# Two attention images per transfer: layouts of keys, offsets, results and matrices, and three picked rows per read, in a deformable attention kernel

## The chip, the cores and the metric

The kernel runs on one core of one Trainium2 chip. Its time is the device time of one execution in microseconds (us); of several executions the median counts. The profile is one further execution under the hardware profiler.

## The reference

A network of two layers works on an image batch of shape (2, 64, 64, 256) in fp32. Each layer adds an attention block and then a mixture-of-experts feed-forward block to its input. The change touches the first layer's attention block alone, which is cut to its core here (B = 2 images, G = 8 groups of HC = 32 channels, K = 9 sampling points):

```python
qkv = _dwconv_nhwc(x @ qkv_w + qkv_b, dw_w, dw_b)      # q, k_map, v_map
mask = jnp.einsum('bchw,oc->bohw', _pconv_nchw(q_nchw, mask_pconv_w), mask_w) + mask_b
for g in range(G):
    off = jnp.einsum('bchw,oc->bohw', _pconv_nchw(q_nchw, off_pconv_w[g]), off_w[g]) + off_b[g] + base[g]
    k_list.append(_flow_warp(k_map[:, sl], off) * mask[:, None])
    v_list.append(_flow_warp(v_map[:, sl], off) * mask[:, None])
attn = softmax(einsum('bgpc,bgpkc->bgpk', qh, k))
out = einsum('bgpk,bgpkc->bgpc', attn, v) @ proj_w + proj_b
```

`base[g]` holds the nine points of a 3 x 3 grid with spacing 2g+1. `_flow_warp` samples a map bilinearly at the pixel's own place plus the offset, with the place clipped to the image. Behind this block follow the first feed-forward block, the second layer's windowed attention and its feed-forward block.

## The kernel before

The kernel is one program. What matters here runs from about 660 to 2880 us of the profiled execution, in two stages.

**Maps.** A depthwise convolution turns the projected q, k and v into maps in DRAM. For q it runs on DVE (`dwconv`), and ACT copies each piece into `q0` or `q1` (L366); SP stores them in `qd` (L368, L370). For v it also runs on DVE, followed by transposes on PE (`ps_t`, L380) and stores to `vd`. For k PE computes it with diagonal weights (`ps_k`, L424), ACT moves the PSUM tile to `km` (L429), and SP stores it in `kd` with a border of repeated columns on both sides (L434, L436). From `q0` and `q1` PE computes the offsets and the mask (`ps_off`, L447 and L448), which ACT copies (L452) and SP stores in `offd` (L453). `offd` has the shape [128, 153, 64]: rows (y, b), then 144 offsets and 9 mask values in the order (g, kx, ky, two), then x.

**Attention.** Because the offsets are smaller than one pixel (a flag `far` tells when they aren't, and another path then runs instead), no gather is needed: every sample is a weighted sum of the 3 x 3 pixels around its grid point. A group g goes through three lanes:

- `group_dots`: SP reads queries and keys (`qt`, L544; `kt`, L554), PE multiplies each column of queries with three columns of keys (`dot`, L564), ACT moves the products to `stage` (L571) and stores them in DRAM as `dots` (L580). `dots` has the shape [y, b, 6, 64, 3, 32]: for each row of queries and image, six blocks (three grid columns by two halves of x), 64 rows of keys, three key columns, 32 queries.
- `group_weights`: SP reads the offsets (`tents`, L632) and picks from `dots` those key rows that each query row needs (`lk`, L660; in `read`, L663, for each of the three grid rows three neighbouring rows). DVE adds the bias (L637), ACT and DVE make the bilinear weights ("tents"), DVE sums the picked products to logits (L694 to L708) and takes the softmax. DVE then makes `wy` (L733), and POOL multiplies it out to the weights `wt` (L740) and stores them along diagonals of a DRAM matrix `wd` (L773). Before it does so it clears that matrix's old diagonals with zeros from `none` (L788, `clean`).
- `group_values`: SP reads the values (`raw`, L859) and DVE spreads them to a block-diagonal `vt` (L861). POOL loads bands of `wd` to one of two buffers `mat` (L868, `load`), PE multiplies `vt` with `mat` into `acc` (L890, `add`), ACT copies a half's result (L899) and stores it in `od` (L903). There are six loads and six adds for a group, four in the last, group 0.

`static_attention` (L456) runs values of one group, weights of the next and dots of the one after that side by side. It puts the steps of the three lanes in one list by a position for each (`lanes`, L503 to L517); a scheduler of the framework then orders each engine's instructions from that list by its own estimates, so the order on an engine isn't that of the source. The groups come in the order 1 to 7, then 0. All DMAs that SP issues share one queue, those of ACT a second and those of POOL a third.[...]

The two images are kept apart in most transfers: one DMA for b = 0 and one for b = 1, as in the load of the matrices:

```python
def load(n):
    h, kx, _ = runs[n]
    for b in range(B):
        for y in range(0, H, BAND):
            lo, hi = band(g, y)
            nc.gpsimd.dma_start(mats[n % 2][H * b + y : H * b + y + BAND, lo:hi], wd[y : y + BAND, b, 2 * kx + h, lo:hi])
```

Such a load fills 16 partitions (BAND = 16), eight of them a matrix. At the end `project_out` reads `od` to `oT` (L931) and multiplies with `proj_w`.

Of the kernel before, what the change touches and what calls it, by code (L numbers as in the profile page):

```python
# [31 lines left out]
P = 128  # L32
# [89 lines left out]

def _shape_constants():
# [9 lines left out]
    grid = np.concatenate([grid.reshape(P, NOFF), np.zeros((P, K), np.float32)], 1)  # L133
# [31 lines left out]
    fold = np.concatenate([fold, own], 1)  # L165
# [15 lines left out]
class Net:  # L181
# [80 lines left out]
    def static_maps(self, maps, sort):  # L262
# [10 lines left out]
        with ExitStack() as ctx:  # L273
# [73 lines left out]
            with tc.tile_pool(name="mpad", bufs=2) as pads, tc.tile_pool(name="mq", bufs=1) as qp, \  # L347
# [12 lines left out]
                for b in range(B):  # L360
                    for j in range(CC):
                        for y in range(0, H, YC):
                            cv = kp.tile([P, YC, W], F32, name="cv")
                            self.dwconv(cv, padded("pad", j, b, y, YC), j, 0, YC)
                            to = q1[:, :, y : y + YC, b] if j else q0[:, 1 : W + 1, 1 + y : 1 + y + YC, b]
                            nc.scalar.copy(to.rearrange("p x y -> p y x"), cv)  # L366
# [43 lines left out]
                for j in range(CC):  # L410
# [5 lines left out]
                    for b in range(B):  # L416
                        km = kp.tile([P, W, H], F32, name="km", bufs=1)
                        for y in range(0, H, 8):
# [3 lines left out]
                            for tap in range(9):  # L422
# [7 lines left out]
                                km[:, :, y : y + 8].rearrange("p x y -> p y x"), ps, AF.Identity,  # L430
                                bias=bias,
                            )
                        to = kd[j * P : (j + 1) * P, b]
                        nc.sync.dma_start(to[:, BORDER : BORDER + W, :], km)  # L434
                        for at, src in ((0, 0), (BORDER + W, W - 1)):
                            nc.sync.dma_start(  # L436
                                to[:, at : at + BORDER, :], km[:, src : src + 1, :].to_broadcast([P, BORDER, H])
                            )
                XO = 8
                for x8 in range(0, W, XO):  # L440
                    off = op.tile([P, NOM, XO], F32, name="off")
                    for x in range(x8, x8 + XO, 2):
# [9 lines left out]
                        nc.scalar.copy(off[:, :, x - x8 : x - x8 + 2].rearrange("p n x -> p x n"), ps)  # L452
# [3 lines left out]
    def static_attention(self, maps, od, far):  # L456
# [7 lines left out]
        with ExitStack() as ctx:  # L464
# [12 lines left out]
            edge = one.tile([P, len(FOLDS) + B], F32, name="edge")  # L477
# [9 lines left out]
            def masks():  # L487

                masks = offd[:, NOFF:, :].rearrange("(y b) (kx ky) x -> b y ky kx x", b=B, kx=3)
                for b in range(B):  # L490
                    for ky in range(3):
                        nc.sync.dma_start(mask[H * b : H * b + H, 3 * ky : 3 * ky + 3, :], masks[b, :, ky])
                v = mask.rearrange("p (ky kx) x -> p ky kx x", ky=3)
                ob = self.row("offb")[:, NOFF:].rearrange("p (kx ky) -> p ky kx", kx=3)
                nc.vector.tensor_tensor(v, v, ob.unsqueeze(3).to_broadcast([P, 3, 3, W]), ALU.add)
                for t in mats + [none, pools["vt"]]:
                    nc.gpsimd.memset(t, 0.0)

            for n in range(-2, G):
                lanes = []  # L500
                if n >= 0:
                    g = ORDER[n]
                    lanes.append((lambda f: 0.12 + 0.88 * f, self.group_values(g, vd, wd[n % 2], mats, none, sums, od, pools)))  # L503
# [7 lines left out]
                if n + 2 < G:  # L511
                    g = ORDER[n + 2]
                    lanes.append((lambda f: 0.95 * f, self.group_dots(g, qd, kd, edge[:, len(FOLDS) :], dots, pools, n < 0)))
# [12 lines left out]
    def group_dots(self, g, qd, kd, own, dots, pools, alone):  # L526
# [22 lines left out]
        def keys(h, dx):  # L549
            box[h, dx] = kt = two.tile([P, XQ + 2, H], F32, name="kt", bufs=3)  # L550
            for j in range(2):
                for b in range(B):
                    x, p0 = BORDER + XH * h + XQ * j + dx, 64 * j + 32 * b
                    nc.sync.dma_start(kt[p0 : p0 + HC], kd[g * HC : (g + 1) * HC, b, x : x + XQ + 2])  # L554
# [45 lines left out]
    def group_weights(self, g, offd, mask, low, edge, s, wd, none, pools):  # L600
# [24 lines left out]
        def offsets():  # L625
            src = offd[:, g * 2 * K : (g + 1) * 2 * K, :].rearrange(
                "(y b) (kx ky two) x -> b y two ky kx x", b=B, kx=3, ky=3
            )
            for b in range(B):
                for i in range(2):  # L630
                    for ky in range(3):
                        nc.sync.dma_start(t5[H * b : H * b + H, 1, i, 3 * ky : 3 * ky + 3, :], src[b, :, i, ky])  # L632

        def bias(i):
            v = t5[:, 1, i].rearrange("p (ky kx) x -> p ky kx x", ky=3)
            ob = self.row("offb")[:, g * 2 * K : (g + 1) * 2 * K].rearrange("p (kx ky two) -> p two ky kx", kx=3, ky=3)
            nc.vector.tensor_tensor(v, v, ob[:, i].unsqueeze(3).to_broadcast([P, 3, 3, W]), ALU.add)  # L637
# [7 lines left out]
        def pick(to, dy, first, blocks, n):  # L645

            for b in range(B):
                y = 0
                while y < H:
                    ky = min(max(y + dy, 0), H - 1)  # L650
                    inside = 0 <= y + dy < H
                    end = min(H, H - dy) if inside else (-dy if dy < 0 and y < -dy else H)
                    m = end - y
                    if m > 16:
                        m -= m % 16
                    src = bass.AP(
                        s.tensor, s.offset + y * stride + b * (stride // B) + first * block + ky * line,
                        [[stride + (line if inside else 0), m], [block, blocks], [1, n * XH]],
                    )
                    nc.sync.dma_start(to[H * b + y : H * b + y + m], src)  # L660
                    y += m

        def read(ky):  # L663
            box[ky] = lk = two.tile([P, 3, 6, 3, XH], F32, name="lk")
            for sy in range(3):
                pick(lk[:, sy].rearrange("p k s x -> p k (s x)"), (ky - 1) * r + sy - 1, 0, 6, 3)

        def read_near():
            flat = two.tile([P, 27 * W], F32, name="ln", tag="lk")
            box["all"] = lk = flat[:, 0 : 25 * W].rearrange("p (y h s x) -> p y h s x", y=5, h=2, s=5)  # L670
            box["l"] = two.tile([P, 3, 6, 3, XH], F32, name="l4", tag="lk")
# [7 lines left out]
        def in_x(ky):  # L679
            tx = t5[:, :, 0, 3 * ky : 3 * ky + 3, :]  # L680
            if near:
                lk, box[ky] = box["all"], box["l"]
                for sy in range(3):
                    out = box[ky][:, sy].rearrange("p (k h) s x -> p h k s x", h=2)
# [8 lines left out]
            for sy in range(3):  # L693
                nc.vector.tensor_tensor(box[ky][:, sy], box[ky][:, sy], tx, ALU.mult)  # L694

        def sum_x(ky, i):
            l = box[ky].rearrange("p y k s x -> p (y k) s x")
# [1792 lines left out]
```

## Time and profile before

| what | value |
| --- | --- |
| median of 3 runs | 5861.54 us (5854.24 to 5861.91) |
| profiled execution | 6110.76 us, span 6109.0 us, granted TensorE clock 0.796 |
| PE, PEld, DVE, ACT, POOL busy in the span | 67%, 47%, 40%, 19%, 24% |
| maps | about 660 to 1190 us |
| attention, dots alone | 1190 to 1425 us |
| attention, all three lanes | 1425 to 2410 us |
| attention, the last groups' values | 2410 to 2880 us |
| output projection | 2880 to 3060 us |
| everything behind (not touched) | 3060 to 6109 us |

The busy shares are means over the whole program, in which stages with quite different limits follow each other. A change in the attention must be read from windows of the profile within it: how busy each engine and the 16 DMA engines are there, what the engines wait for, and in which order POOL, SP and ACT issue their work. An engine's idle time costs nothing unless the end of the stage depends on it.

The groups that carry the stage, from the groups of instructions between 1190 and 2880 us (line, engine, operation, names, shapes, count; busy us and mean ns of one; idle us before them and what ended the idle time):

```profile
L890 PE MATMUL acc<-mat,vt 128*64 128x192 f32 (+2 forms) x3680 | 491.7, 439 | 255.9 <-DMA mat<-wd 182.0 <-DMA wd<-wt 32.8 <-DVE vt L861 26.1
L564 PE MATMUL dot<-kt,qt 64*128 64x192 f32 x2944 | 408.4, 411 | 479.1 <-ACT stage L571 320.8 <-DVE stage L571 61.7 <-DMA kt<-kd 43.5
L868 POOL DMA_DIRECT2D mat<-wd x368 | 179.8, 494 | 590.5 <-PE acc L890 390.5 <-DMA wd<-none 88.1 <-DMA mat<-wd 61.4
L773 POOL DMA_DIRECT2D wd<-wt x170 | 167.6, 991 | 143.6 <-issue 49.4 <-DMA wd<-wt 36.4 <-DMA mat<-wd 31.0
L740 POOL TENSOR_TENSOR wt<-tents,wy 128x192 f32<-128x192 f32 x216 | 128.5, 626 | 198.6 <-DVE wy L733 189.3 <-DMA wd<-wt 9.0
```

### The profile page before, as it was taken

The page shows a single profiled execution, that of the slowest core. Times are in us where ns is not written, and L with a number is a line of the kernel's source. Part 1 is how long each engine was busy: PE and PEld are TensorE (multiplying, and loading weights), DVE is VectorE, ACT ScalarE, POOL GpSimd, SP SyncE. Part 2 cuts the span into 40 slices and gives each one's busy share as a digit, 9 for nine tenths or more (in the row PEclk, how much of TensorE's full clock was granted, in tenths as well). Part 3 has the DMA queues.
Part 4 walks back from the last instruction along what each step waited for, and adds up shares of the span by engine and source line. Part 5 has one row for each costly group of instructions (what it writes and reads, how often), then busy time and mean ns, then how long its engine had stood idle before and what let it go on. Part 6 is the DMA issues. An engine that isn't in the chain of part 4 may idle for free. (4 is left out here: it accounts for less than half of the span.)

```text
span 6109.0 us, 63383 instructions
## 1 busy us (share of the span) xinstructions
PE 4115.2 (67%) x22123; PEld 2876.5 (47%) x22123; DVE 2467.9 (40%) x5464; ACT 1154.1 (19%) x2302; POOL 1470.7 (24%) x1792
## 2 busy tenths in 40 slices
PE   7877688758265566354625680499947877769982
PEld 4655245745243444233412340388824444458872
DVE  6788985043121202220423473011155555532223
ACT  2110121122122222000100000122213343322210
POOL 1000001123342232443155414300062111110025
PEclk8776799868577777677867795699967888879986
DMA  6333367968678897787320001577621000058875
GB/s 179 97 102 113 99 171 148 66 152 179 126 159 175 176 188 155 120 142 126 84 13 4 4 2 64 173 225 223 194 86 40 22 21 22 21 184 263 263 235 159
DMA packets 775144, 759.72 MB, mean 124 GB/s; under 512 B 443959, under 2 KB 658935, under 8 KB 759317
## 3 DMA queue, kind: packets, MB, share of 16 engines
q1 hardware_dynamic: 576992, 412.37, 26.8%
q0 software_dynamic: 87008, 200.21, 16.9%
q10 hardware_dynamic: 110804, 142.87, 8.1%
q8 instruction: 182, 2.98, 0.2%
q14 instruction: 158, 1.29, 0.1%
HBM read 461.72 MB, written 296.60 MB: 124 GB/s over the span
## 5 line engine op out<-in xcount | busy, mean ns | idle before, releaser
L564 PE MATMUL dot<-kt,qt 64*128 64x192 f32 x2944 | 408.4, 411 | 479.1 <-ACT stage L571 320.8
L890 PE MATMUL acc<-mat,vt 128*64 128x192 f32 (+2 forms) x3680 | 491.7, 439 | 255.9 <-DMA mat<-wd 182.0
L564 PEld LDWEIGHTS dot<-kt,qt 64*128 64x128 f32 x2944 | 355.5, 235 | 535.7 <-ACT stage L571 340.5
L1658 PE MATMUL ps_h<-xgT,w1t 128*128 128x256 f32 x2240 | 545.0, 391 | 41.8 <-DVE xgT L1653 17.6
L1391 PE MATMUL ps<-oh,ol 128*128 128x512 f32 (+1 forms) x864 | 363.2, 584 | 240.8 <-issue 150.5
L1666 PE MATMUL ps_y<-w2t,hT 128*128 128x256 f32 x2240 | 513.9, 383 | 7.5 <-issue 4.4
L890 PEld LDWEIGHTS acc<-mat,vt 128*64 128x64 f32 x3680 | 310.3, 163 | 441.1 <-issue 318.1
L1658 PEld LDWEIGHTS ps_h<-xgT,w1t 128*128 128x128 f32 x2240 | 417.6, 193 | 122.8 <-DVE xgT L1653 26.2
L1666 PEld LDWEIGHTS ps_y<-w2t,hT 128*128 128x128 f32 x2240 | 430.0, 192 | 69.1 <-issue 5.2
L1661 ACT ACTIVATE hT<-ps_h,b1t 128x256 f32<-128x256 f32 x560 | 258.6, 473 | 846.4 <-PE ps_h L1658 756.7
L571 ACT COPY stage<-dot 128x384 f32<-128x384 f32 x640 | 269.5, 495 | 745.6 <-PE dot L564 295.2
L1669 DVE TENSOR_TENSOR y<-ps_y,b2t 128x256 f32<-128x256 f32 x280 | 118.8, 424 | 648.2 <-PE ps_y L1666 493.7
L1391 PEld LDWEIGHTS ps<-oh,ol 128*128 128x128 f32 x864 | 179.6, 212 | 424.0 <-issue 319.9
L868 POOL DMA_DIRECT2D mat<-wd x368 | 179.8, 494 | 590.5 <-PE acc L890 390.5
L424 PE MATMUL ps_k<-padk,diag 128*128 128x512 f32 x576 | 266.1, 621 | 76.4 <-issue 50.2
L260 DVE SCALAR_TENSOR_TENSOR cv<-pad,colt,cv 128x2048 f32<-128x2048 f32 x128 | 293.8, 2347 | 1.3
L2286 POOL DMA_INDIRECT xs<-tn,sloti x128 | 124.2, 971 | 638.9 <-DVE slot L2284 592.7
L1753 POOL DMA_INDIRECT back<-ys,back_row x128 | 123.3, 964 | 621.9 <-DVE run L2271 548.6
L1275 PE MATMUL psc<-oh,ol 128*128 128x64 bf16 x1792 | 235.0, 305 | 55.6 <-DVE oh L1273 55.6
L1275 PEld LDWEIGHTS <-ol 128*128 128x128 bf16 x1792 | 224.9, 148 | 94.0 <-issue 54.9
L333 PE MATMUL ps_q<-xT,wq 128*128 128x512 f32 x384 | 217.7, 708 | 44.5 <-ACT stage L337 33.2
L1651 PE MATMUL ps_x<-ident,xg 128*128 128x128 f32 x560 | 85.0, 275 | 225.4 <-DMA xg<-xs 225.4
(401 smaller groups left out, 6112.7 us busy)
## 6 DMA issues: line engine op xcount, KB each, us to landing
w1t<-in_W SPq DMA_DIRECT2D x140, 512.0 KB
w2t<-in_W SPq DMA_DIRECT2D x140, 512.0 KB
xg<-xs SPq DMA_DIRECT2D x140, 256.0 KB
ys<-y ACTq DMA_DIRECT2D x140, 256.0 KB
kt<-kd SPq DMA_DIRECT2D x184, 144.0 KB
pr<-stage SPq DMA_DIRECT2D x16, 1584.0 KB
mat<-wd POOLq DMA_DIRECT2D x112, 192.0 KB
mat<-wd POOLq DMA_DIRECT2D x64, 288.0 KB
```

The lines of the kernel that those rows point to most:

```text
L260: nc.vector.scalar_tensor_tensor(out, src, w, out, ALU.mult, ALU.add)
L333: nc.tensor.matmul(ps.rearrange("p a b -> p (a b)"), lhsT=wq[:, k, c * P : (c + 1) * P], rhs=xT[:, k, :], start=(k == 0), stop=(k == CC - 1),)
L424: nc.tensor.matmul(ps.rearrange("p a b -> p (a b)"), lhsT=diag[:, tap, :], rhs=pad[:, at : at + 8, tap % 3 : tap % 3 + W], start=(tap == 0 ...
L564: nc.tensor.matmul(ps[jj][:, i, :], lhsT=qt[at, i0 + i].rearrange("p y b -> p (y b)"), rhs=kt[at, i0 + i : i0 + i + 3, :].rearrange("p s y ...
L571: (nc.vector.tensor_copy if alone and jj else nc.scalar.copy)(box["d"][:, :, :, x : x + 2], ps[jj].rearrange("p i (s y) -> p y s i", s=3),)
L868: nc.gpsimd.dma_start(mats[n % 2][H * b + y : H * b + y + BAND, lo:hi], wd[y : y + BAND, b, 2 * kx + h, lo:hi])
L890: nc.tensor.matmul(sums[h][64 * q : 64 * q + 64, j - 2 + a : j - 2 + c, :].rearrange("p x y -> p (x y)"), lhsT=vt[:, r + 1 + XH * h + XQ * ...
L1275: nc.tensor.matmul(psc, lhsT=ol[:, :, j], rhs=oh[:, :, j], start=(c1 == 0), stop=(c1 == NW - 1),)
L1391: nc.tensor.matmul(psf[:, c : c + m], lhsT=ol, rhs=ohf[:, c : c + m], start=(start and j == 0), stop=(stop and j == n - 1),)
L1658: nc.tensor.matmul(ps, lhsT=w1t[:, k, f * P : (f + 1) * P], rhs=xT[:, k, :], start=(k == 0), stop=(k == CC - 1),)
L1661: nc.scalar.activation(hT[:, f, :], ps, AF.Gelu, bias=b1t[:, f : f + 1])
L1666: nc.tensor.matmul(ps, lhsT=hT[:, f, i * P : (i + 1) * P], rhs=w2t[:, f, :], start=(f == 0), stop=(f == NF - 1),)
```

## The change

The layouts are changed so that one transfer serves both images, with 32, 48 or 64 as its outermost count:

- `kd` and `od` become [g, b, channel, x, y] (they were [channel, b, x, y]), so that one read of keys or one store of results covers 64 partitions, both images. `kd` is therefore written in four parts of 32 channels.
- The rows of a matrix in `mat`, and those of `raw` and `vt`, interleave the images (y outer, b inner), so that one load covers 16 rows of both: 32 partitions. The values are spread to the block-diagonal `vt` by multiplying with a column `odd` of zeros and ones on all 128 partitions, in place of copies of 64.
- The 153 offsets are sorted on the host into the order (g, two, ky, kx) (`_offset_order`), and the biases with them, so that offsets of a group come in one read for each image, 4,608 B a row, where there were six. The two bias additions become one.
- `lk` is laid out [block, row, column, x] so that three neighbouring rows of a grid row are picked by one read of 1,152 B runs, where all three lie inside the image; rows at the edge are still read one by one.
- ACT's copies of q, km and the offsets now write in order and read with strides, where they read in order and wrote with strides.

```diff
-                            nc.scalar.copy(to.rearrange("p x y -> p y x"), cv)
+                            nc.scalar.copy(to, cv.rearrange("p y x -> p x y"))
...
-                                km[:, :, y : y + 8].rearrange("p x y -> p y x"), ps, AF.Identity,
+                                km[:, :, y : y + 8], ps.rearrange("p y x -> p x y"), AF.Identity,
...
-                        to = kd[j * P : (j + 1) * P, b]
-                        nc.sync.dma_start(to[:, BORDER : BORDER + W, :], km)
+                        for g in range(4):
+                            to, part = kd[4 * j + g, b], km[g * HC : (g + 1) * HC]
+                            nc.sync.dma_start(to[:, BORDER : BORDER + W, :], part)
...
             for j in range(2):
-                for b in range(B):
-                    x, p0 = BORDER + XH * h + XQ * j + dx, 64 * j + 32 * b
-                    nc.sync.dma_start(kt[p0 : p0 + HC], kd[g * HC : (g + 1) * HC, b, x : x + XQ + 2])
+                x = BORDER + XH * h + XQ * j + dx
+                nc.sync.dma_start(
+                    kt[64 * j : 64 * j + 64].rearrange("p x y -> p (x y)"),
+                    kd[g, :, :, x : x + XQ + 2].rearrange("b c x y -> (b c) (x y)"),
+                )
...
             for b in range(B):
-                for i in range(2):
-                    for ky in range(3):
-                        nc.sync.dma_start(t5[H * b : H * b + H, 1, i, 3 * ky : 3 * ky + 3, :], src[b, :, i, ky])
+                nc.sync.dma_start(t5[H * b : H * b + H, 1].rearrange("p i k x -> p (i k x)"), src[b])
...
         def read(ky):
-            box[ky] = lk = two.tile([P, 3, 6, 3, XH], F32, name="lk")
+            box[ky] = lk = two.tile([P, 6, 3, 3, XH], F32, name="lk")
+            dy = (ky - 1) * r
+            y0, y1 = max(0, 1 - dy), min(H, H - 1 - dy)
+            pick(lk.rearrange("p k y s x -> p k (y s x)"), dy - 1, 0, 6, 9, y0, y1)
             for sy in range(3):
-                pick(lk[:, sy].rearrange("p k s x -> p k (s x)"), (ky - 1) * r + sy - 1, 0, 6, 3)
+                for lo, hi in ((0, y0), (y1, H)):
+                    pick(lk[:, :, sy].rearrange("p k s x -> p k (s x)"), dy + sy - 1, 0, 6, 3, lo, hi)
...
-                raw = pools["one"].tile([P, 32, HC], F32, name="raw", tag="raw")
-                nc.sync.dma_start(raw[:, 0:n, :], vd[g].rearrange("b y x c -> (b y) x c")[:, x0 + x : x0 + x + n, :])
+                nc.sync.dma_start(
+                    raw[:, 0:n, :].rearrange("p x c -> p (x c)"),
+                    vd[g, :, :, x0 + x : x0 + x + n].rearrange("b y x c -> y b (x c)"),
+                )
                 for b in range(B):
-                    nc.vector.tensor_copy(vt[H * b : H * b + H, x : x + n, b, :], raw[H * b : H * b + H, 0:n, :])
+                    nc.vector.tensor_scalar(vt[:, x : x + n, b, :], raw[:, 0:n, :], odd[:, b : b + 1], None, ALU.mult)
 
         def load(n):
             h, kx, _ = runs[n]
-            for b in range(B):
-                for y in range(0, H, BAND):
-                    lo, hi = band(g, y)
-                    nc.gpsimd.dma_start(mats[n % 2][H * b + y : H * b + y + BAND, lo:hi], wd[y : y + BAND, b, 2 * kx + h, lo:hi])
+            for y in range(0, H, BAND):
+                lo, hi = band(g, y)
+                nc.gpsimd.dma_start(
+                    mats[n % 2][B * y : B * (y + BAND), lo:hi].rearrange("p h s x -> p (h s x)"),
+                    wd[y : y + BAND, :, 2 * kx + h, lo:hi].rearrange("y b h s x -> (y b) (h s x)"),
+                )
...
-                for b in range(B):
-                    x, p0 = XH * h + XQ * q, 64 * q + 32 * b
-                    nc.scalar.dma_start(od[g * HC : (g + 1) * HC, b, x : x + XQ], o[p0 : p0 + HC])
+                x = XH * h + XQ * q
+                nc.scalar.dma_start(
+                    od[g, :, :, x : x + XQ].rearrange("b c x y -> (b c) (x y)"),
+                    o[64 * q : 64 * q + 64].rearrange("p x y -> p (x y)"),
+                )
```

`pick` takes a first and a last row (`y0`, `y1`) in addition and sets rows that touch the image's edge apart; the bodies of `in_x`, `sum_x`, `in_y` and `sum_y` address the new layout of `lk` with the same number of operations. The path for large offsets is adapted to the new layouts; it doesn't run with these inputs.

## The prediction

> **What bounds the kernel now.** The chain that ended last reaches back only through the last few hundred microseconds, the feed-forward matmuls (ps_h 4%, ps_y 4%), which the change leaves alone. So the first attention had to be read by itself. The table by windows comes first (busy us and count of each engine, then granted clock, share of the 16 DMA engines, GB/s):
>
> ```profile
> core 0: us, PE busy (x) PEld busy (x) DVE busy (x) ACT busy (x) POOL busy (x), PEclk, DMA share, GB/s
> 1190.00:1425.00 235.00, 121.37 (x792) 102.98 (x794) 105.32 (x160) 50.40 (x102) 66.53 (x64) 0.68 0.65 150
> 1800.00:2000.00 200.00, 107.67 (x774) 79.37 (x776) 39.08 (x48) 46.42 (x105) 54.91 (x78) 0.73 0.79 166
> 2000.00:2200.00 200.00, 109.63 (x814) 81.44 (x810) 40.17 (x52) 50.42 (x116) 52.17 (x82) 0.75 0.85 181
> 2200.00:2400.00 200.00, 114.13 (x820) 82.89 (x816) 44.36 (x56) 48.61 (x110) 57.63 (x86) 0.74 0.84 173
> 2600.00:2880.00 280.00, 143.25 (x1034) 97.10 (x1029) 55.31 (x74) 7.85 (x8) 119.20 (x205) 0.75 0.79 124
> ```
>
> No engine is busy for 60% of a stretch; the DMA engines are, at 0.79 to 0.85. Over 1190 to 2880 us (the attention) their share makes about 0.79 x 1690 = 1335 us. The DMA view of 1425 to 2880 says which queues hold them (q0 is POOL's, q1 SP's, q10 ACT's):
>
> ```profile
> DMA packets 125162, 224.22 MB, mean 154 GB/s; under 512 B 97421, under 2 KB 98954, under 8 KB 114297
> q0 software_dynamic: 40572, 98.92, 43.4%
> q1 hardware_dynamic: 74276, 60.29, 20.7%
> q10 hardware_dynamic: 10233, 63.94, 16.0%
> ```
>
> The two timelines show how that becomes time: SP needs 33.40 us to issue 11 reads where an issue costs 0.3 us[...], and ACT 24.67 us for four stores, after which its copy is named late by 25.68 us. [...]
>
> ```profile
> 2053.27 33.40 SPq L660 DMA_DIRECT2D lk<-dots  x11
> ...
> 2083.44 24.67 ACTq L580 DMA_DIRECT2D dots<-stage  x4
> 2108.21 0.88 ACT L571 COPY stage<-dot 128x384 f32<-128x384 f32 x2 [25.68 <-DMA lk<-dots]
> ```
>
> The list of waits from 1190 to 2880 us names who pays: the loads of mat wait for acc (a buffer comes free), acc waits for mat, and POOL's weights wait for DVE.
>
> ```profile
> POOL mat L868 <- PE acc L890: 390.5, 24, 60.4
> PE dot L564 <- ACT stage L571: 320.8, 35, 30.5
> POOL wt L740 <- DVE wy L733: 189.3, 8, 127.4
> PE acc L890 <- DMA mat<-wd: 182.0, 10, 57.8
> ```
>
> So the stage is a mixture: DMA time, and a serial loop in which POOL issues loads, makes the next group's weights and issues loads again.
>
> [...]packets of 12,288 B of mat<-wd (16 partitions) take 1,252 ns in the mean, 9.8 GB/s an engine or 157 for 16; packets of the same size of dots<-stage (32 partitions) take 652 ns, 18.8 GB/s an engine. [...]384 B of lk in 33 ns, 256 B of tents in 34 ns, 4,608 B of kt in 298 ns.
>
> **The change, part by part.** All in the profiled execution's time (6,110.76 us, span 6,109.0), which stands 4.3% above the median 5,861.54; its sum is multiplied by 0.96 at the end.
>
> Mats. 368 loads to 16 partitions become 184 to 32, same bytes. Their packets add up to 7,505 engine-us, 469 us of 16 engines. If they reach the stores' rate, the factor is 652/1252 = 0.52[...]; two neighbouring old loads lie 64 partitions apart and may already overlap, so I take 0.65: 469 x 0.35 = 164 us less. Bounds: 0.52 (225) and 1.0 (0[...]). POOL issues 184 x 0.494 = 91 us less, at places where it mostly waits for acc: nothing.
>
> Picks. lk has 49,664 packets of 384 B at 33 ns, 1,624 engine-us. The 40 joint reads of 48 rows, with their remainders, carry 1,152 B; ACT's packets of 1,024 B have 60 ns in the mean. Part of the rows stay single (edges), so I take 370 engine-us off: 23 us (0 to 50). tents and mask: 20,864 packets at 34 ns = 704 engine-us become about 1,024 packets of 4,608 B at 298 ns = 305 and 256 of 2,304 B: 25 us less. SP issues fall by 80 of tents, 92 of kt, about 40 of lk: at 0.35 us 74 us of an issuer[...]; it counts inside the share below.
>
> Keys, od. kt goes from 32x1152 to 64x1152: same packets of 4,608 B[...]: 0. The od stores likewise. kd<-km is split in 16 and 32 pieces of 32 partitions[...]; before 1190 us, beside PE work that ends later: 0, at worst 10.
>
> Sum of DMA time saved: 164 + 23 + 25 = 212 of 1,335. At 0.80 to 0.85 share not all becomes time: stretches that wait for DVE's wy (189.3 us) or for POOL don't shrink. I take 0.7: -148 us. Bounds 0.35 (-74) and, with the mats at 0.52, 0.9 (-245).
>
> POOL's order. The built orders differ where the diff is silent. Before, the weights of the next group stand between the loads of this one (load 3, wt x9, wd x8, load 4, wt, load 5, wt, wd x14, clean x8). The timeline of POOL in one such passage:
>
> ```profile
> 2572.49 1.91 POOL L868 DMA_DIRECT2D mat<-wd  x4 [6.37 <-PE acc L890]
> ...
> 2582.38 5.03 POOL L740 TENSOR_TENSOR wt<-tents,wy 128x192 f32<-128x192 f32 x9
> ...
> 2598.52 3.94 POOL L868 DMA_DIRECT2D mat<-wd  x8 [0.63 <-DMA wd<-wt]
> ...
> 2608.16 0.54 POOL L868 DMA_DIRECT2D mat<-wd  x1 [0.66 <-PE acc L890]
> ...
> 2637.24 8.22 POOL L788 DMA_DIRECT2D wd<-none x8
> 2645.45 0.53 POOL L868 DMA_DIRECT2D mat<-wd  x1
> ```
>
> After, all six loads of a group come first in groups 0 to 4, and the weights follow: what started at 2582.38 would start after the load at 2608 with its seven other issues, at some 2612, 30 us later, and the work from 2582 to 2645 without its 12 us of loads takes 51: the next group's load 0 at 2663, 18 us later. Five passages: 90. Against it, loads 4 and 5 come earlier, and in one passage POOL waits for wy up to 127.4 us in any case, which hides the shift. I take +45 (0 to 100). What is queued behind the late weights: the next group's six loads, and on PE its acc.
>
> PE's order in the maps stage. Before, PE does 72 more ps_k while DVE finishes q (until 826):
>
> ```profile
> 802.67 1.21 PE L447 MATMUL ps_off<-w_off,q 128*128 128x153 f32 x8
> 808.65 17.71 PE L424 MATMUL ps_k<-padk,diag 128*128 128x512 f32 x36 [4.77 <-DMA padk<-pr]
> ```
>
> After, only 39 ps_k stand before the first ps_t, which needs DVE's first v (about 838), and on ACT the fifth q copy (770 before) stands ahead of the two km copies (753) that free ps_k's PSUM. So 33 ps_k of 0.95 us are left over: +31, less idle time that ps_k x36 and ps_t cost in before (about 35 us between 826 and 1176) and that other work may now fill. I take +25 (-5 to +45) for the start of the dots; what follows is the stage without values (1190 to 1425), with PE busy in 121 of 235 us, so it is not made up there.
>
> Small edits. vt: 48 copies of 64 partitions (632 ns) become multiplications on 128 (nearest row: 128x1152 in 871 ns): 12 us on a DVE that is 20% busy, nothing on the path; cost if the cover goes, the 12. One memset less: 5.2 us on POOL, before its first weights. bias: as many elements, half the instructions. ACT's q, km and off copies write in order and read strided; the trace has only the strided write (1.9 ns an element[...]), so between -15 and +15 of a queue that DVE feeds: 0.
>
> Sum: -148 + 45 + 25 = -78; x 0.96 = -75; 5861.5 - 75 = 5787.
>
> **Rivals.** First, the DMA gain dominates: the mats do reach 0.52 and the moved weights hide behind DVE's wy: (225 + 48) x 0.7 = 191 less, +10 left for the orders: 5861 - 0.96 x 181 = 5688; with 0.9 in place of 0.7 it ends at 5636. For it speak the acc waits for mat<-wd (182.0); against it that acc waits mostly for things in a chain.
>
> Second, slower: POOL's serial passage decides. If POOL, and not the DMA, sets the group's length, faster mats only make it wait sooner for weights that now begin after load 5: five passages at 20 to 25 us (+100 with load 0's own), the late dots +45, DMA only 212 x 0.42 = -90: +55, x 0.96, 5914. It decides from the point at which the weights' delay, per group, exceeds what the six loads save (about 164/8 = 20 us). The 390.5 us of POOL waiting for acc speak for it, the 0.85 share against it.
>
> Third, the change doesn't do what it says: the mats stay at 9.8 GB/s an engine since the software queue or their spread bounds them. Then 48 us of DMA time are left, x 0.7 = -34, against +70: +36, or 5896.
>
> **How the numbers follow.** Forecast (DMA gain larger than both orders' cost, 5787, own range 5720 to 5850) 0.43; first rival 0.18; slower by POOL's passage 0.20; mats not faster 0.14; the rest, near no change, 0.05. What a measurement can tell from no change is about 0.2%, 12 us. Faster 0.59, same 0.06, slower 0.35. The range reaches from the first rival (5640) to the second (5925).
>
> **What would show it.** Right: mat packets of 12,288 B well under 1,000 ns; q0's share down by a third; lk and tents issues without 30 us stops; first dot at about 1200 to 1215; in POOL's timeline, weights after the last load of each group. Wrong: mat packets still at 1,200 ns; the wait of acc for mat<-wd replaced by one for wd<-wt or wd<-none; groups as far apart as now (load 0 to load 0 about 200 us).

## The result and the profile after

The changed kernel takes 5817.39 us (median of 4 runs, 5815.83 to 5828.35) against 5858.92 us before: the ratio is 0.9934 (95% interval 0.9917 to 0.9951), 41.5 us less. The forecast was 5787 us, within 5640 to 5925.

The profiled execution of the changed kernel has a span of 5816.6 us, 292 us less than the one shown of the kernel before, and most of that is not the change: the one-hot matmuls behind the attention, which the change leaves alone, ran from 3122 to 3479 us here and from 3137 to 3675 us there. The chips that served the runs differ: the kernel before took 5854 to 5859 us on some and 6135 to 6163 us on others. So below, ratios are formed only with runs of the kernel before on the same chip, and stages are compared only up to the end of the attention, where a second profile of the kernel before (the first experiment) is the better partner.

The windows of the changed kernel's attention (busy us and count of each engine, then granted clock, DMA share, GB/s):

```profile
core 0: us, PE busy (x) PEld busy (x) DVE busy (x) ACT busy (x) POOL busy (x), PEclk, DMA share, GB/s
1282.00:1514.00 232.00, 119.88 (x784) 103.08 (x784) 103.75 (x157) 51.94 (x106) 47.08 (x54) 0.69 0.64 156
1900.00:2100.00 200.00, 121.05 (x920) 84.81 (x920) 49.46 (x59) 50.94 (x115) 73.35 (x97) 0.79 0.78 177
2300.00:2500.00 200.00, 127.61 (x936) 90.93 (x936) 50.73 (x58) 51.52 (x117) 65.05 (x90) 0.79 0.82 203
2640.00:2853.00 213.00, 125.87 (x892) 79.33 (x892) 45.05 (x66) 7.84 (x8) 80.64 (x130) 0.76 0.67 147
```

and its queues with all lanes running, 1514 to 2853 us:

```profile
DMA packets 79777, 220.45 MB, mean 165 GB/s; under 512 B 40661, under 2 KB 53207, under 8 KB 69055
...
q0 software_dynamic: 37744, 99.09, 36.3%
q1 hardware_dynamic: 33032, 58.63, 18.6%
q10 hardware_dynamic: 8928, 61.75, 18.1%
```

A packet is the unit in which the profile records a transfer: those of lk have 384 B in the kernel before, and here 384 B (6,824 of them) or 1,152 B (14,280). POOL's queue (q0) moves the same bytes in a smaller share of a shorter time (36.3% of 1339 us against 43.4% of 1455 us). SP's share (q1) hardly falls, although it has less than half the packets. The first line of the windows begins at 1282 us: that is the first dot, and it was 1198 us before. PE's timeline shows where the start went:

```profile
753.70 0.42 PE L455 MATMUL ps_off<-w_off,q 128*128 128x153 f32 x2
793.23 6.82 PE L455 MATMUL ps_off<-w_off,q 128*128 128x153 f32 x34 [39.11 <-ACT q L373]
823.84 35.95 PE L431 MATMUL ps_k<-padk,diag 128*128 128x512 f32 x78 [23.80 <-ACT km L436]
```

Eighteen offset matmuls (36 records) stand in front. The first reads a border column of q0 and runs; the second needs ACT's sixth copy of q (at 789.36 us) and idles PE for 39 us. Then ps_k waits 24 us for its PSUM, which ACT empties only after the next copy of q. In the kernel before, one offset matmul ran at this point, and then PE had ps_k to do:

```profile
747.56 0.42 PE L447 MATMUL ps_off<-w_off,q 128*128 128x153 f32 x2
754.36 48.47 PE L424 MATMUL ps_k<-padk,diag 128*128 128x512 f32 x108 [6.38 <-ACT km L429]
```

In the changed kernel PE was busy for 22 us of 753 to 838; before, for 67 of 748 to 826.

The waits of the changed attention (total us, times, longest):

```profile
DVE lk L701 <- DMA lk<-dots: 486.2, 40, 43.6
POOL mat L876 <- PE acc L901: 466.8, 29, 41.3
...
PE dot L572 <- ACT stage L579: 318.5, 31, 67.5
...
POOL wt L747 <- DVE wy L740: 176.6, 6, 131.2
PE acc L901 <- DMA mat<-wd: 174.7, 12, 44.4
```

PE still waits for mat about as long as before (174.7 us, 182.0 before). POOL waits longer for a free buffer (466.8, 390.5 before), and DVE waits longer for the picked products; before, that line was

```profile
DVE lk L694 <- DMA lk<-dots: 191.2, 30, 31.5
```

The loads are faster. That the products' way through DRAM (stage, dots, lk, wy) is what comes late next is a reading of these waits, not yet a test; DVE's wait costs nothing unless wy comes late by it.

### The profile page after: what moved, and what is told of

It reads as the page before. It is cut to its first block, busy times and chain, and to the rows that moved or that the text cites. A ratio compares the mean times of both kernels' runs of the same rounds, so it can differ in the third digit from the quotient of the medians.

```text
span 5816.6 us, 62877 instructions
## 1 busy us (share of the span) xinstructions
PE 4034.6 (69%) x22123; PEld 2831.9 (49%) x22123; DVE 2473.1 (43%) x5456; ACT 1131.5 (19%) x2302; POOL 1385.2 (24%) x1607
## 5 line engine op out<-in xcount | busy, mean ns | idle before, releaser
L572 PE MATMUL dot<-kt,qt 64*128 64x192 f32 x2944 | 394.2, 401 | 448.4 <-ACT stage L579 318.5
L901 PE MATMUL acc<-mat,vt 128*64 128x192 f32 (+2 forms) x3680 | 497.3, 439 | 220.1 <-DMA mat<-wd 174.7
L572 PEld LDWEIGHTS dot<-kt,qt 64*128 64x128 f32 x2944 | 339.8, 228 | 509.8 <-ACT stage L579 341.7
L1407 PE MATMUL ps<-oh,ol 128*128 128x512 f32 (+1 forms) x864 | 328.3, 543 | 95.3 <-DVE oh L1400 95.3
L701 DVE TENSOR_TENSOR lk<-lk,tents 128x576 f32<-128x576 f32 x63 | 46.2, 757 | 497.7 <-DMA lk<-dots 486.2
```

Source lines behind the costliest of these rows:

```text
L572: nc.tensor.matmul(ps[jj][:, i, :], lhsT=qt[at, i0 + i].rearrange("p y b -> p (y b)"), rhs=kt[at, i0 + i : i0 + i + 3, :].rearrange("p s y ...
L901: nc.tensor.matmul(sums[h][64 * q : 64 * q + 64, j - 2 + a : j - 2 + c, :].rearrange("p x y -> p (x y)"), lhsT=vt[:, r + 1 + XH * h + XQ * ...
L1407: nc.tensor.matmul(psf[:, c : c + m], lhsT=ol, rhs=ohf[:, c : c + m], start=(start and j == 0), stop=(stop and j == n - 1),)
```

## The experiments

Per kernel, from the traces: first dot, attention (first dot to last copied result), DMA time in it (the sum of the packets' times, divided by the 16 DMA engines), that of the mats (packets of 7,680 B and more in POOL's queue), the mean 12,288 B packet of mats, and the ratio to the kernel before with its interval. The first profile of the kernel before has 1198 us, 1672, 1311, 469 and 1252 ns in these columns.

| kernel | first dot | attention | DMA | mats | packet | ratio |
| --- | --- | --- | --- | --- | --- | --- |
| before, again | 1203 us | 1695 us | 1306 us | 477 us | 1270 ns | 1 |
| changed | 1282 | 1571 | 1131 | 329 | 870 | 0.9934 (0.9917-0.9951) |
| kd_only | 1279 | 1697 | 1314 | 479 | 1269 | 1.0137 (1.0116-1.0158) |
| mats_only | 1193 | 1576 | 1139 | 324 | 855 | 0.9808 (0.9786-0.9831) |
| kd_fix | 1234 | 1574 | 1141 | 324 | 870 | 0.9852 (0.9824-0.9880) |
| picks_only | 1199 | 1702 | 1305 | 465 | 1258 | 1.0020 (1.0010-1.0031) |
| mats_stride2 | 1195 | 1550 | 1098 | 301 | 799 | 0.9776 (0.9756-0.9795) |
| mats_wide | 1201 | 1539 | 1016 | 215 | 566 | 0.9725 (0.9701-0.9749) |
| wide16 | 1201 | 1559 | 1110 | 313 | 828 | 0.9775 (0.9745-0.9804) |
| wide_v3 | 1200 | 1538 | 1013 | 222 | 589 | 0.9776 (0.9756-0.9797) |
| wide_w3 | 1194 | 1639 | 1013 | 210 | 558 | 0.9887 (0.9865-0.9910) |
| stores_sp | 1193 | 1602 | 1001 | 222 | 577 | 0.9863 (0.9832-0.9893) |
| stores_pool | 1198 | 1479 | 985 | - | 614 | 0.9653 (0.9621-0.9686) |

wide16, wide_v3 and wide_w3 ran beside a kernel before of 5853.53 us, all others but the changed one beside 6135 to 6163 us; a few tenths of a per cent between these two sets are not told apart here. In stores_pool the stores share POOL's queue with the mats, so the mats' time isn't separated, and its packet mean includes stores.

**The kernel before once more.** No edit.

> The kernel before once more, for a second profile: its first profiled execution was 4.3% longer than its median, the changed kernel's was not, so the two can't be compared stage by stage without this. If the excess lay behind the attention (the single longest difference is in the one-hot matmuls from 3137 to 3675 us, 181 us), the span is near 5860 us and the attention again runs from about 1198 to 2870 us (within 25 us). If the excess was spread, the attention ends some 80 us earlier than 2870, and the changed kernel then gained nothing in it.

It took 6176 us, not about 5860: on this chip the median of the kernel before was 6163 us, so the excess belongs to the chip and not to one execution. The attention ran from 1203 to 2898 us and the one-hot matmuls from 3167 to 3722 us (357 us long in the changed kernel's profile, 555 here), so most of the excess lies behind the attention. The attention ends 28 us later than in the first profile, just over the expected 25, and is 23 us longer: this is the size by which two profiles of one kernel differ.

**The split of kd alone.** With the tile's shape and the address of the keys' reads to match; the borders follow the same loop.

```diff
-                        to = kd[j * P : (j + 1) * P, b]
-                        nc.sync.dma_start(to[:, BORDER : BORDER + W, :], km)
+                        for g in range(4):
+                            to, part = kd[4 * j + g, b], km[g * HC : (g + 1) * HC]
+                            nc.sync.dma_start(to[:, BORDER : BORDER + W, :], part)
```

> Only the write of kd is split (four parts of 32 channels, new layout, keys still read in 32 partitions); everything else as before. In the program PE's order in the maps stage becomes that of the changed kernel, and POOL's order stays. Theory (the split moves PE's and ACT's order and so delays the dots): first dot at about 1280 us instead of 1198, time 5859 + 60 to 85 = about 5935. Rival (the dots came late through another part of the change: the strided copies of ACT, the joint reads): first dot within 15 us of 1198, time within 15 us of 5859.

6246.14 against 6162.84 us, +83 us; first dot at 1279, attention unchanged. Its timeline on PE has the changed kernel's two stops:

```profile
786.74 7.52 PE L448 MATMUL ps_off<-w_off,q 128*128 128x153 f32 x34 [38.34 <-ACT q L366]
817.55 36.56 PE L424 MATMUL ps_k<-padk,diag 128*128 128x512 f32 x78 [23.30 <-ACT km L429]
```

So the split alone makes the late start, and all of it reaches the end. ACT's copies are as before here, so they are not the cause. Slow transfers of the split are not seen either: ACT's km copies wait 11.7 us for kd<-km in the maps stage here, and 19.7 in the second profile of the kernel before. What differs is the order that the scheduler made of twelve issues in place of three. The experiment kd_fix below keeps the split and changes that order.

**The mats alone.** The interleaved load, raw, vt and `odd` of the changed kernel, put into the kernel before:

```diff
-            for b in range(B):
-                for y in range(0, H, BAND):
...
-                    nc.gpsimd.dma_start(mats[n % 2][H * b + y : H * b + y + BAND, lo:hi], wd[y : y + BAND, b, 2 * kx + h, lo:hi])
+                    mats[n % 2][B * y : B * (y + BAND), lo:hi].rearrange("p h s x -> p (h s x)"),
+                    wd[y : y + BAND, :, 2 * kx + h, lo:hi].rearrange("y b h s x -> (y b) (h s x)"),
```

> Only the matrices, values and block-diagonal vt interleave the two images (loads of 32 partitions, 184 of them); everything else as before. PE's order in the maps stage stays, POOL's order becomes about that of the changed kernel (all loads of a group, then the next group's weights). Theory (the mats bring nearly all of the gain): packets of 12,288 B at about 870 ns instead of 1,252, time 5859 - 100 = about 5760 (5730 to 5790). Rival (the gain comes from fewer and larger SP transfers, mats are hidden): 5845 to 5860.

125 us less, more than the 100 expected, with packets of 855 ns. The attention is as short as the changed kernel's (1576 and 1571 us), so joint keys, picks, offsets and results together add nothing to it that can be seen. Of 167 us of DMA time saved, 119 became time: 0.71 (against the first profile of the kernel before, 97 of 172: 0.56). One passage of POOL and DVE shows what a group waits for now:

```profile
1747.26 6.54 POOL L789 DMA_DIRECT2D wd<-none  x4 [17.07 <-issue]
1753.82 5.50 POOL L741 TENSOR_TENSOR wt<-tents,wy 128x192 f32<-128x192 f32 x9
...
1802.61 12.32 POOL L774 DMA_DIRECT2D wd<-wt  x13
...
1858.26 3.46 POOL L871 DMA_DIRECT2D mat<-wd  x7
```

```profile
1739.73 1.21 DVE L721 TENSOR_REDUCE red<-lg 128x64 f32<-128x576 f32 x1 [15.39 <-ACT lg L716]
...
1743.15 0.76 DVE L734 TENSOR_TENSOR wy<-tents,lg 128x576 f32<-128x576 f32 x1
```

The last add of the group before ended at 1744, when wy was just made. Then POOL makes weights and zeros until 1858, when the first loads start, and PE has no values to add until 1881. In six of eight groups the first wt starts as soon as wy is there; in the kernel before it came 20 to 70 us after wy in the groups from the fourth on, behind loads.

**The start repaired.** In the changed kernel, all four main parts of kd first, and their borders from POOL's queue:

```diff
+                            nc.sync.dma_start(kd[4 * j + g, b, :, BORDER : BORDER + W, :], km[g * HC : (g + 1) * HC])
+                        for g in range(4):
...
-                            nc.sync.dma_start(to[:, BORDER : BORDER + W, :], part)
...
-                                nc.sync.dma_start(
+                                nc.gpsimd.dma_start(
```

> The changed kernel, with the border columns of kd written from POOL's queue after the four main parts, in place of SP's. In the program PE then again does 72 ps_k before most of the offsets, as in the kernel before. Theory (late start of the dots is a loss of its own): first dot at 1200 to 1225 us instead of 1282, time 5817 - 55 to 80 = about 5750. Rival (the start is made up for later, since the stage has slack against its DMAs): first dot as early, but time within 20 us of 5817.

The first dot came at 1234 us, not 1200 to 1225, so the order was only in part that of the kernel before: between its first and last offset matmul PE idled 82 us here, 51 before, 131 in the changed kernel. The ratio is 0.9852 against 0.9934 for the changed kernel: some 48 us, as much as the start moved (1282 to 1234). The attention behind it is of the same length. The late start is a loss of its own; nothing makes it up.

**The picks alone.** `read`, `pick` and the layout of lk as in the changed kernel, the rest as before.

> Only the picks are joint (three rows of a grid row in one read of 1,152 B runs, lk laid out for it); everything else as before, POOL's and PE's orders as before but for one passage. Theory (the picks bring nothing: in the changed kernel a packet of 1,152 B takes 91 ns, nearly the 99 ns of three of 384 B): attention from first dot to last value within 20 us of the 1,672 to 1,694 us of before, ratio 0.996 to 1.004. Rival (SP's fewer issues shorten the stage): DVE's wait for lk falls below 150 us and the ratio is 0.985 to 0.994.

12 us slower (1.0010 to 1.0031), as the theory allowed. DVE's wait for lk did not fall below 150 us, as the rival wanted, but was 226.6. A packet of 1,152 B takes 100 ns here, 91 in the changed kernel; three of 384 B take 99. DMA time of lk stayed at 101 to 104 us.

**Sixteen partitions with a stride of two.** On mats_only:

```diff
-            for y in range(0, H, BAND):
+            for b in range(B):
+                for y in range(0, H, BAND):
...
-                    mats[n % 2][B * y : B * (y + BAND), lo:hi].rearrange("p h s x -> p (h s x)"),
+                        mats[n % 2][B * y + b : B * (y + BAND) : B, lo:hi].rearrange("p h s x -> p (h s x)"),
```

> The kernel before with the images interleaved in mat, raw and vt as in mats_only, but each load still carries one image: 16 partitions, every second of 32, so 368 loads. POOL's order is exactly that of the kernel before (the next group's weights between the loads). [...]packets of 12,288 B at 850 to 900 ns as in mats_only, though there are as many loads as before; and if POOL's order costs nothing, since the weights wait for DVE's wy in either order, the ratio to before is again 0.975 to 0.985; if the order costs the 45 us that I took for it, the ratio is 0.970 to 0.976. Rival (a load is faster[...] because there are half as many): packets at 1,200 ns or more and a ratio of 0.995 to 1.005.

As many loads, as many partitions and the same order on POOL as in the kernel before, yet packets take 799 ns (1270 there). It is the place of the partitions, and neither their number nor that of the loads, that made the mats slow. The attention is 26 us shorter than in mats_only, about as much as two profiles of one kernel differ; the intervals of the ratios just overlap.

**Rows on every fourth partition.** On mats_only, with `raw` read in four pieces and `odd` set to match:

```diff
-                    mats[n % 2][B * y : B * (y + BAND), lo:hi].rearrange("p h s x -> p (h s x)"),
+                    mats[n % 2][y // BAND : P : H // BAND, lo:hi].rearrange("p h s x -> p (h s x)"),
```

> As mats_only, but the 32 rows of a load lie on every fourth partition of all 128 (partition 4(2(y mod 16) + b) + y div 16)[...]; raw is read in four pieces of 32 partitions for the same order of rows. Theory[...]: packets of 12,288 B at 700 to 800 ns in place of 855, and some 15 to 40 us less than mats_only (ratio 0.974 to 0.979). Rival[...]: packets within 5% of 855 ns, ratio 0.979 to 0.985, or slightly worse through 60 to 120 more reads of raw.

566 ns, well below the 700 to 800 that I expected, and a ratio of 0.9725, just below the range. The median packet takes 467 ns. But of 123 us of DMA time less than mats_only only 37 came off the attention (0.3; by the ratios some 51 us, 0.4): here DMA time counted for less than in the step before.

**POOL's order, three ways.** wide16 loads each image by itself on every eighth partition; wide_v3 and wide_w3 move a lane's place in the common list, wide_v3 that of the values (below), wide_w3 that of the weights (0.3 f in place of 0.04 + 0.8 f):

```diff
-                    lanes.append((lambda f: 0.12 + 0.88 * f, self.group_values(
+                    lanes.append((lambda f: 0.3 + 0.7 * f, self.group_values(
```

> The rows as in mats_wide, but each load carries one image again: 16 partitions, every eighth of 128[...], 368 loads, and so POOL's order of the kernel before. Theory (POOL's order costs about 25 us, which mats_stride2 saved against mats_only[...]): packets of 12,288 B at 570 to 700 ns, ratio to before 0.966 to 0.972, below mats_wide's 0.9725. Rival (the 0.3% between mats_stride2 and mats_only had another cause, for instance their packets of 799 and 855 ns): ratio at or above 0.9725.

> mats_wide with the values' steps placed later in the common list (0.3 + 0.7f in place of 0.12 + 0.88f), so that POOL again has weights of the next group between the loads, with 184 loads. If POOL's order is worth about 25 us: ratio 0.966 to 0.972. If it isn't, or if later values cost as much: 0.972 to 0.980.

> mats_wide with the weights' steps placed earlier (0.3f in place of 0.04 + 0.8f): POOL has the weights after the second of six loads, so DVE must have wy early. If POOL's order alone limited the groups: ratio 0.960 to 0.970. If wy (SP's reads of lk, DVE) limits them, POOL waits for wy with the group's loads queued behind it, and the ratio is 0.975 or more.

wide16 went as its rival said: 0.9775, with packets of 828 ns. Whether loads of the two images in a row help each other it doesn't show: its loop issues the four loads of one image in a row, each one partition further than the last, so the two images' loads seldom stand next to each other. Its attention is 20 us longer than mats_wide's, with POOL's order of the kernel before.

wide_v3 has both the fast packets and weights between loads, and the same attention as mats_wide (1538 and 1539 us). Either POOL's order is worth nothing there, or the values, which come later, cost as much as it gains; the run doesn't part the two. What the order is worth with mats_only's packets stays open, between 0 and 26 us.

wide_w3 lost 100 us, as the second half of its expectation said. But the cause given there, POOL's wait for wy with loads queued behind it, can't be all: wide_v3 (first line) waits longer for wy than wide_w3 (second line) and loses nothing.

```profile
POOL wt L741 <- DVE wy L734: 352.1, 6, 142.9
POOL wt L741 <- DVE wy L734: 324.5, 9, 142.8
```

PE's waits for vt are longer in wide_w3 (136.1 us, 73.1 in wide_v3), and so are DVE's for lk (456.8 and 314.7). Which of them costs the 100 us stays open.

**Who issues the stores of dots.** On wide_v3, one word in `store`: `nc.sync` or `nc.gpsimd` in place of `nc.scalar`. In the profile's records each issue names a semaphore that its transfer completes on. From 1190 to 2880 us of the kernel before, SP's 768 transfers and ACT's 253 complete on semaphores 100 to 107, and POOL's 584 on 111 to 118, 73 on each; 643 of SP's issues and 166 of ACT's wait for the semaphore that they themselves complete on.

> wide_v3 with the stores of dots issued by SP in place of ACT. In the traces SP's and ACT's transfers take turns on eight completion semaphores (100 to 107): an issue on one engine waits until the turn before it on that semaphore has landed, so ACT stops behind SP's reads (copies of stage behind lk: 156 us in mats_wide, the longest 57) and SP behind ACT's stores. With the stores on SP, ACT issues only the results. Theory (ACT's stops hold up PE's dots and with them the stage): ACT's waits for lk nearly vanish, attention from first dot to last value 1,537 - 30 to 80 us, ratio 0.963 to 0.972. Rival (the same order of turns only moves to SP, which then stands behind PE's dots with its reads of lk and keys): attention 1,537 us or more, ratio 0.976 to 0.99.

> wide_v3 with the stores of dots issued by POOL, whose transfers have semaphores of their own (111 to 118), so that neither SP nor ACT shares turns with the stores. Theory (the shared turns limit the stage): ratio below 0.972. Rival (POOL in its order is the bound: 184 more issues of 0.5 us and more, and stores that wait for stage ahead of loads and weights): ratio above 0.985, POOL's waits for ACT's stage above 100 us.

The two go opposite ways: 1602 us on SP, 1479 on POOL, from 1538 on ACT. With the stores on SP the theory failed and the rival came true (0.9863): ACT's waits for lk did nearly vanish (16.4 us, 101.6 in wide_v3), and the attention still grew. So ACT's stops by themselves were not the limit. That POOL, which has the most to issue, is the best place speaks against issue time as the limit. With SP, POOL's wait for wy is the longest of all:

```profile
POOL wt L741 <- DVE wy L734: 451.8, 7, 113.5
```

and with POOL it is

```profile
POOL wt L741 <- DVE wy L734: 201.0, 13, 46.3
...
POOL dots L581 <- ACT stage L572: 146.0, 20, 32.2
```

The theory's range for stores_pool is met; its rival's wait of POOL is there too (146.0 us), but costs less than the move saves. stores_pool has the lowest ratio of all: 5935.19 us against 6134.9, 0.9653, while the changed kernel's was 0.9934.

## Why the prediction was right, and where it was not

The sign held, and the mats were the main gain, through faster packets (870 ns, 1270 before); 41.5 us came of the 74.5 forecast. The range reached from well below to above no change, so that a time inside it says little; the terms say more. By stage, with the second profile of the kernel before, the start of the attention cost 54 us more than its term and the attention itself gained 21 more. The first difference is clear. The second is not: the two profiles of the kernel before differ by 23 us in the attention, and against the first one the changed kernel gained 101 us, nearly the 103 forecast. The second profile's sum, -124 + 79 = -45, lies closer to the measured -41.5.

1. Mats: 164 us of DMA time were to go, with a factor of 0.65 between 0.52 and 1.0. 148 went (477 to 329), a factor of 0.69. mats_stride2 and mats_wide show that the spread over partitions was the cause: on 16 neighbouring partitions a packet took 1270 ns, on 32 neighbouring ones 855 (mats_only) and 870 (the changed kernel), on every second of 32 799, on every eighth of 128 828 (wide16), and on every fourth of 128 566. Set against 1270 ns, the rate was 1.5 to 1.6 times as high in the first four and 2.2 times in the last, beside other traffic. Why the spread counts, no run here shows. But the reason for taking 0.65 and not 0.52 was a slip: two loads in a row do not lie 64 partitions apart. The trace has them in the order of their sizes 7,680, 9,216, 9,216 and 7,680 B a row, the four bands of one image, 16 partitions apart. That 0.65 came near 0.69 is luck so far.
2. Picks and offsets: 23 and 25 us of DMA time. lk gained 7 (picks_only none), because a packet of three times the length takes three times as long. The offsets gained some 11: their 256 B packets took 36 us before and 2 after, and the 4,608 B packets 98 and 120. All edits other than mats and lk have 20 of 175 us between them, and that is an upper bound: mats_only, which leaves them out, lost 14 us outside the mats as well. In time, they gave nothing that shows.
3. The share that becomes time: 0.7 was taken, and 0.71 measured (mats_only; the changed kernel as a whole: 124 of 175 us). Against the first profile of the kernel before both are 0.56, so the agreement is closer than the measurement. It is no constant: the next 123 us, in mats_wide, brought 0.3 to 0.4. The reading behind it, that no engine is busy for 60% of a stretch, came from a table that left out a stretch in which PE is busy for 73%:

```profile
1425.00:1600.00 175.00, 128.38 (x932) 89.07 (x928) 38.53 (x48) 50.11 (x117) 64.56 (x83) 0.81 0.82 165
```

4. POOL's order: +45 was probably too much. The order did change as described, but in the changed kernel the first wt of a group waits for wy and not for the loads ahead of it: it starts at most 25 us after wy, and in five of eight groups at once. The working looked at POOL's queue alone; the sentence that DVE's wy may hide the shift was the right one. The run that keeps the order of before with packets as fast (mats_stride2) leaves 0 to 26 us for it.
5. The start of the attention: the step that failed. +25 (-5 to +45) was taken; it was +79, outside the bounds. Two assumptions did it. "kd<-km is split ... 0, at worst 10" priced the transfers, and the split's cost is the order that follows from it (kd_only: +83 us of time with nothing but kd's layout and its writes changed). And the orders were compared by counting the ps_k that are left over (+31), without asking what the 18 offset matmuls in front of them need: the sixth copy of q, 39 us later, and after it the PSUM of ps_k, 24 us. The idle time that was to be filled was not filled: PE idled 51 us between its first offset matmul and its last before, 131 us after.
6. What stopped the issuers, the instruction records tell in part. At ACT's four stores at 2083.44 us it was the turns of SP's and ACT's transfers on the eight semaphores 100 to 107. ACT's last store, at 2107.81, waited for turn 102, and SP's read that had this turn before it landed at 2107.79. Of SP's 33.40 us, only some 11 are such waits, for earlier reads of its own; the other 22 are the issues themselves, nine of which take 1.3 to 3.8 us in place of 0.3, for a reason that stays open. In the changed kernel the turns stop SP as well (start us, engine, transfer, semaphore waited for, semaphore that it completes on):

```
1515.77  SP   lk<-dots     100  100
1541.11  ACT  dots<-stage  109  101
1543.84  SP   lk<-dots     101  101
```

SP's read needs turn 101, which ACT's store had before it, and that store was issued only when its products were there: 28 us, in 20 of which (1520 to 1540) no packet of q1 ran. The sizes show that the read belongs to group 2 (spacing 5, six rows at the image's edge) and the store to group 3 (spacing 7, 32 rows of keys), so the read doesn't wait for the store's data. That relieved turns are what stores_pool gained by is not proved, since that run moves the issue too; stores_sp, in which ACT's stops went and time was lost, shows that it matters who is stopped.

Of the signs named ahead, the faster packets came (870 ns), and so did the weights behind a group's last load. The first dot at 1200 to 1215 us did not (1282), nor did the stops of lk's issues go (28 us above), and q0's share fell by a sixth, not by a third.

Of the rivals, the one in which mats stay slow falls with the packets of 870 ns. The one in which POOL's passage decides needed a longer attention; it became shorter by 101 to 124 us. The one in which the DMA gain dominates would have come nearer without the split of kd: mats_only is 125 us faster, of which the late start hid two thirds.

## What to carry to other kernels

When a layout is changed for one stage, look at what the new layout makes of the stage that writes it: here a split of a store that looked free cost 83 us through the order of a scheduler, two thirds of what the rest had gained. When two orders of instructions are compared, follow each instruction that moved forward to the input it waits for, rather than count those that moved back. And where a load is slow, vary the places of its partitions before its size: with interleaved rows, loads of one image (mats_stride2, 799 ns a packet) gained what the joint ones did (mats_only, 855 ns). Take a second profile of the kernel before, too: without it, a difference of 23 us between two profiles of one kernel would have been read as a gain or a loss.

## What was not expected of the hardware

- In these runs a load's packets were fast or slow by its own spread over partitions. In the kernel before, two loads in a row fill 32 neighbouring partitions between them, and a packet of 12,288 B took 1270 ns; one load of such 32 partitions took 855 (mats_only), one of every second of them 799 (mats_stride2), and one of every fourth of all 128 took 566 (mats_wide).
- Packets of 384 B and of 1,152 B of lk, read from scattered rows, had about the same price per byte (33 ns before, and 91 ns in the changed kernel to 100 in picks_only).
- ACT's copies from PSUM were quicker when they wrote in order and read with strides: km took 686 ns in place of 1151, the offsets 438 in place of 718. The q copies from SBUF hardly changed: 3856 ns, 3934 before.
